# Three narrow products of a decoder kernel, with the narrow operand loaded in four quarters of TensorE's columns

## The chip, the cores and the metric

The kernel runs on one core of a Trainium2 chip, in one launch, in float32 almost throughout. The metric is the device time of an execution in microseconds (us). Three executions of the kernel before took 2194.0, 2196.74 and 2199.11 us; the median is 2196.74 us.

TensorE (PE in the profile) holds one operand of a matmul as weights and streams the other past it. VectorE is DVE, ScalarE is ACT, GpSimd is POOL, and SP is the engine whose queue issues most DMAs. A float32 matmul of this kernel leaves two records of PE in the trace, each with its own load of weights (PEld); a transpose through PE leaves one.

## The reference, cut to what matters

The decoder has two layers of three blocks, each followed by a residual sum and a layer norm. x is 8 x 256 x 512, that is 2048 tokens of 512 features. The change touches three products with a very narrow operand:

```python
# L0_attn: differential attention; one mean square per token and head, 16 heads of 32 features
attn = attn1 - lambda_full * attn2
attn = attn * jax.lax.rsqrt(jnp.mean(attn * attn, axis=-1, keepdims=True) + EPS) * ln_w
attn = attn * (1.0 - LAMBDA_INIT)
return attn @ Wo.T

# L0_ffn: mixture of experts, 8 experts, the best two of each token
logits = h @ router_w.T                      # 512 -> 8
vals, idx = lax.top_k(softmax(logits), 2)

# L1_ffn: attention with one key and value head chosen for each token, 16 heads
gating = jax.nn.softmax(x @ W_gate.T, axis=-1)   # 512 -> 16
idx = jnp.argmax(gating, axis=-1)
k_shared = jnp.einsum('bth,bthd->btd', indicator, k)
```

Between them stand a long convolution (L0_xattn), a causal attention in chunks (L1_attn) and a cross attention (L1_xattn), which the change leaves alone.

## The kernel before, in words

Tokens lie in 16 tiles of 128 (`x[t]`), features in four blocks of 128 (KB = 4). A product with 512 features is four matmuls that add up in PSUM, one for each block of features. Where tokens are to be the output's partitions, the transposed tokens are the weights and the other operand is streamed; this is how the three narrow products are done before: 128 tokens are loaded as weights, and 4, 8 or 16 columns are streamed.

The stages follow each other: differential attention (to about 486 us), long convolution (to 786), experts (to 1132), the self attention (to 1504), cross attention (to 1847), routed attention (to the end).

**The order in the two attention stages.** `causal_attention` (L1102 on) writes the order of PE, DVE, ACT and POOL out by hand. Its unit of work is one batch of 256 tokens and four heads. For each unit, PE makes scores (`ps_q`, L1158), ACT copies them (L1167), POOL masks them (L1169), DVE takes the row maxima (L1178); nine or five units later PE makes the scores again, transposed (`ps_k`, L1221 and L1230), ACT takes the exponential (`pT`, L1238), POOL masks (L1239) and adds (L1249), and PE multiplies by the values and by ones (`ps_pv`, L1264 and L1274); DVE takes the reciprocal of the sums (`rsum`, L1282) and multiplies (L380, L383 or L1288). The two kinds of scores share one PSUM tile (tag sc), so PE may start the next `ps_q` only when ACT has taken the exponential of the last `ps_k`. Between these, `fill` puts in pieces of other work up to a budget, at costs written into the code (0.86 for a 128x512 product's matmul, 0.45 for four transposes, 0.4 for a set of norm sums): projections, and what `finish` hands in after each batch. A slot's places are "start", then `ps_q`, a first fill, `ps_pv`, "mid", `ps_k`, two more fills, the row maxima on DVE, and "end".

**The head norms** are in `finish` of the differential attention (L435). For the first seven of the eight batches, ACT squares the gathered output (L480), and `norms(i)`, one for each of the two token tiles, makes four matmuls of 128 tokens by the 4 columns of `quad` (L449; `quad` has a one for each of the four groups of 32 features). DVE scales and adds epsilon into `rr` (L453), POOL takes the power -1/2 (L461), ACT widens (L457), PE transposes it (`pt_rr`, L471), DVE multiplies (L477). The last batch goes another way (L392), which is not changed.

**The routing logits** are in `token_tile` (L727) of `route`. Tokens are routed in two halves of eight tiles. For a tile, four transposes (`pt_c`, L731), an ACT copy (L737), the moments on DVE and POOL, the norm of the tile before, and four matmuls of 128 tokens by 8 router columns into `ps_r` (`project`, L172), with an ACT copy into `raw` (L744). `choose`, `send` and `table` then pick the experts, scatter the tokens and make the table of blocks. The first half runs in the middle of the long convolution, where the tile framework's scheduler sets the order; the second runs among the first three blocks of the experts (L1019 on), in an order written by hand. `ps_r`, `pt_c` and the blocks' own transposes (L195) share the two buffers of the pool `ps_t`.

**The gates** of the routed attention are in `gates` (L1698): for each group of four token tiles, 16 matmuls of 128 tokens by 16 columns of W_gate into `ps_g`, then a DVE copy (L1706), the softmax and the choice of the head (L583 to L605, L1710). Ahead of them `turned_group` transposes the group's tokens into `xT`, tile by tile (`pt`, L195; copies by ACT, L196). The `key` of each token block needs the choice.

## Time and profile before

| | |
|---|---|
| median of the runs, us | 2196.74 (2194.0 to 2199.11) |
| the profiled execution, us | 2205.52 |
| its span, first to last instruction, us | 2203.7 |
| mean granted TensorE clock | 0.971 |
| PE busy, us (share of the span) | 2054.0 (93%) |
| DVE, POOL, ACT busy, us | 1275.9, 826.9, 605.1 |
| PE's records of `ps_ss` (L449), `ps_r`, `ps_g` | 112, 128, 128 |

The profile is of one execution. A line of its lists has the source line, engine, operation, output and inputs by their names in the program, and shapes; times in the lists by time are start and duration in us, and what stands in brackets is idle time of that engine before the instruction and what ended it. A matmul's duration is longer than its distance from the next, since matmuls are pipelined; costs of PE are therefore read as distances between starts. In lists by stage, "PEclk" is the granted share of TensorE's clock.

### The profile page before, as it was taken

The page shows a single profiled execution, that of the slowest core. Times are in us where ns is not written, and L with a number is a line of the kernel's source. Part 1 is how long each engine was busy: PE and PEld are TensorE (multiplying, and loading weights), DVE is VectorE, ACT ScalarE, POOL GpSimd, SP SyncE. Part 2 cuts the span into 40 slices and gives each one's busy share as a digit, 9 for nine tenths or more (in the row PEclk, how much of TensorE's full clock was granted, in tenths as well). Part 3 has the DMA queues.
Part 4 walks back from the last instruction along what each step waited for, and adds up shares of the span by engine and source line. Part 5 has one row for each costly group of instructions (what it writes and reads, how often), then busy time and mean ns, then how long its engine had stood idle before and what let it go on. Part 6 is the DMA issues. An engine that isn't in the chain of part 4 may idle for free. (4 is left out here: it accounts for less than half of the span.)

```text
span 2203.7 us, 36445 instructions
## 1 busy us (share of the span) xinstructions
PE 2054.0 (93%) x15296; PEld 1264.8 (57%) x15296; DVE 1275.9 (58%) x1923; ACT 605.1 (27%) x773; POOL 826.9 (38%) x918
## 2 busy tenths in 40 slices
PE   8989999889999998999968999999999999999995
PEld 6646655544453464555545665656877875545543
DVE  4677777658888962222235756556344343576777
ACT  4545555410010021111113333330110110333342
POOL 2667777646557622000034544333000000142343
PEclk9989999989999999999979999999999999999998
DMA  6899802235133153131141201002100100000000
GB/s 220 331 384 381 311 1 69 78 93 186 34 115 120 29 172 121 60 144 63 43 144 30 77 20 58 2 1 96 36 22 20 39 0 1 1 11 11 11 18 32
DMA packets 110035, 197.61 MB, mean 90 GB/s; under 512 B 7088, under 2 KB 30768, under 8 KB 109872
## 3 DMA queue, kind: packets, MB, share of 16 engines
q1 hardware_dynamic: 104752, 178.49, 23.3%
q0 software_dynamic: 5120, 16.78, 2.2%
q8 instruction: 123, 2.02, 0.4%
q14 instruction: 40, 0.33, 0.0%
HBM read 93.54 MB, written 112.20 MB: 93 GB/s over the span
## 5 line engine op out<-in xcount | busy, mean ns | idle before, releaser
L1282 DVE RECIPROCAL rsum<-ps_pv 128x256 f32<-128x256 f32 x128 | 224.5, 1754 | 243.7 <-PE ps_pv L1274 243.4
L172 PE MATMUL ps_y<-kv,wt 128*128 128x512 f32 x640 | 281.1, 597 | 4.5 <-POOL kv L526 3.8
L1238 ACT ACTIVATE pT<-ps_k 128x1536 f32<-128x1536 f32 x128 | 185.8, 1451 | 286.0 <-PE ps_k L1230 282.1
L1178 DVE TENSOR_REDUCE neg<-rows 128x12 f32<-128x1536 f32 x128 | 223.0, 1742 | 54.1 <-POOL rows L1169 54.0
L1169 POOL TENSOR_SCALAR_AFFINE_SELECT rows<-rows 128x1024 f32<-128x1024 f32 x128 | 141.5, 1105 | 246.8 <-ACT rows L1167 246.5
L1167 ACT COPY rows<-ps_q 128x1536 f32<-128x1536 f32 x128 | 184.3, 1440 | 179.4 <-PE ps_q L1158 130.2
L1239 POOL TENSOR_SCALAR_AFFINE_SELECT pT<-pT 128x1024 f32<-128x1024 f32 x128 | 141.1, 1103 | 242.6 <-ACT pT L1238 242.4
L172 PEld LDWEIGHTS ps_y<-kv,wt 128*128 128x128 f32 x640 | 120.3, 191 | 153.6 <-issue 135.2
L1249 POOL TENSOR_TENSOR pT<-pT 128x512 f32<-128x512 f32 x112 | 145.7, 1301 | 9.3
L183 PE MATMUL ps_f<-xT,w_l1a 128*128 128x256 f32 x512 | 129.2, 400 | 12.2 <-ACT xT L196 12.2
L1084 POOL DMA_INDIRECT w_l1x<-ys,slots x32 | 32.7, 1023 | 279.8 <-DMA ys<-y_m 272.1
L183 PE MATMUL ps_t<-w_l1f,xT 128*128 128x512 f32 x256 | 121.9, 611 | 0.0
L183 PEld LDWEIGHTS ps_f<-xT,w_l1a 128*128 128x128 f32 x512 | 96.9, 197 | 33.8 <-ACT xT L196 14.3
L999 PE MATMUL po_m<-dn,hT 128*128 (+1 forms) x216 | 104.4, 621 | 12.0 <-ACT hT L992 10.5
L140 POOL TENSOR_SCALAR rstd<-bn_mv 128x1 f32<-128x1 f32 x80 | 16.6, 207 | 216.2 <-DVE bn_mv L146 208.1
L1274 PE MATMUL ps_pv<-pT,ones_v 128*32 128x256 f32 (+1 forms) x1152 | 84.7, 376 | 7.2 <-POOL pT L1249 7.0
L564 DVE TENSOR_REDUCE yc<-z 128x64 f32<-128x512 f32 x128 | 86.1, 674 | 6.2 <-POOL w_l1a L565 5.7
L981 DVE TENSOR_TENSOR h_b<-h_b,pg 128x352 f32<-128x352 f32 x36 | 18.8, 521 | 101.3 <-ACT h_b L980 101.3
L1158 PE MATMUL ps_q<-kz,qT 32*128 32x128 f32 x1536 | 62.2, 292 | 15.2 <-ACT pT L1238 13.3
L1158 PEld LDWEIGHTS ps_q<-kT,qT 32*128 32x128 f32 x1536 | 49.2, 188 | 44.4 <-issue 21.2
L1158 PEld LDWEIGHTS ps_q<-kz,qT 32*128 32x128 f32 x1536 | 49.8, 190 | 41.0 <-ACT pT L1238 26.2
L183 PE MATMUL ps_f<-xT,w_l 128*128 128x256 f32 x256 | 71.2, 406 | 0.9 <-POOL w_l L273 0.7
(326 smaller groups left out, 3768.7 us busy)
## 6 DMA issues: line engine op xcount, KB each, us to landing
xs<-zero SPq DMA_DIRECT2D x8, 4352.0 KB
ys<-zero SPq DMA_DIRECT2D x8, 4352.0 KB
filters<-in_L_xattn_k SPq DMA_DIRECT2D x4, 2560.0 KB
first_h<-xs SPq DMA_DIRECT2D x36, 256.0 KB
ys<-y_m SPq DMA_DIRECT2D x36, 256.0 KB
gu<-in_L_ffn_gate_up_proj SPq DMA_DIRECT2D x3, 2816.0 KB
wt<-filters SPq DMA_DIRECT2D x32, 256.0 KB
x<-in_x SPq DMA_DIRECT2D x16, 256.0 KB
```

The costliest lines, as they stand in the source:

```text
L172: nc.tensor.matmul(ps, lhsT=lhsT(k), rhs=rhs(k), start=(k == 0), stop=(k == n - 1))
L183: nc.tensor.matmul(ps[0], lhsT=lhsT(k), rhs=rhs(k), start=(k == 0), stop=(k == KB - 1))
L564: nc.vector.tensor_reduce(yc[:, lb], z, AX.X, ALU.add)
L999: nc.tensor.matmul(po, lhsT=hT[:m, i, :], rhs=dn[i][:m, bass.ds(e, 1), :], start=(i == 0), stop=(i == len(FCH) - 1),)
L1158: nc.tensor.matmul(block[:, s, j, :], lhsT=q(rows, c, b * S + i * P, P), rhs=k(rows, c, b * S + keys * P, P), start=True, stop=True,)
L1167: nc.scalar.copy(d.rearrange("p j s k -> p s j k"), block)
L1169: nc.gpsimd.affine_select(out=rows, in_=rows, compare_op=ALU.is_ge, fill=-FAR, base=0, pattern=[[0, 8], [-1, P]], channel_multiplier=1,)
L1178: return lambda: nc.vector.tensor_reduce(neg[u // upb % 2][:, :, :, c], d, AX.X, ALU.max, negate=True)
L1238: nc.scalar.activation(p[:, 0:3].rearrange("p j s q -> p s j q"), block, AF.Exp)
L1239: nc.gpsimd.affine_select(out=p[:, 0:2].rearrange("p j s q -> p (j s) q"), in_=p[:, 0:2].rearrange("p j s q -> p (j s) q"), compare_op=ALU ...
L1249: nc.gpsimd.tensor_tensor(p[:, 3], p[:, 1], p[:, 2], ALU.add)
L1282: nc.vector.reciprocal(r, ps[:, 1, :])
```

## The change

Each of the three products swaps its operands. The narrow operand becomes the weights, 32 columns wide, and the tokens are streamed. The four blocks of features go to four quarters of TensorE's columns and so to four quarters of the PSUM partitions (`ps[32 * k : 32 * k + 32]`), each matmul by itself instead of adding up. The sums over the blocks are made later: ACT or DVE copies the 128 rows out of PSUM, PE transposes them back to tokens, and DVE adds the four blocks (gates, logits) or picks them apart (norm sums, where the four blocks are different heads).

- Gates: one set of four 512-token matmuls for each group of four tiles, an ACT copy (`gpart`), four transposes placed after the first of the query products, and a DVE reduction. The second query product moves ahead of the key products. The budget cost is 0.86 and 0.45 in place of 0.8.
- Logits: one set for four tiles, after the fourth and the eighth tile of each half; the transposes and the reduction (`logits`) come at the start of the fifth tile and of `choose`. The 16 small copies of ACT become four of 128x512.
- Norm sums: one set of four 256-token matmuls for a batch (cost 0.7 in place of twice 0.4), DVE makes `means` in their place, and `norms` makes two transposes and a DVE copy at the "end" of the same slot. A 32-column version of `quad` (`quads`) is made by DVE for every batch.
- Where 32 columns reach past the end of a narrow operand, zeros stand behind it: a POOL memset behind the router weights, a DVE memset behind W_gate, whose load now goes ahead of the load of W_qkv on SP.

```diff
+    def columns_by_block(ps, dst, w, n, rhs):
+        for k in range(KB):
+            nc.tensor.matmul(
+                ps[32 * k : 32 * k + 32, :],
+                lhsT=w[:, n * k : n * k + 32],
+                rhs=rhs(k),
+                start=True,
+                stop=True,
+            )
+        nc.scalar.copy(dst, ps)
+
+    def sum_of_blocks(dst, pt, parts):
+        for i in range(pt.shape[1]):
+            nc.tensor.transpose(pt[:, i, :], parts[:, i * P : (i + 1) * P], ident)
+        n = dst.shape[2]
+        nc.vector.tensor_reduce(
+            dst, pt.rearrange("p t (k r n) -> p t r n k", k=KB, n=n)[:, :, 0], AX.X, ALU.add
+        )
...
-            def norms(i):
-                ps = pools.tile([P, H0], F32, tag="mm", name="ps_ss")
+            quads = work.tile([P, 32], F32, tag="quads", name="quads", bufs=1)
+            nc.vector.tensor_copy(
+                quads.rearrange("p (r t) -> p r t", r=8), quad.unsqueeze(1).broadcast_to([P, 8, 4])
+            )
+            means = work.tile([P, S], F32, tag="means", name="means", bufs=1)
+            def sums():
+                ps = pools.tile([P, S], F32, tag="mm", name="ps_ss")
                 for k in range(KB):
                     nc.tensor.matmul(
-                        ps[:, 4 * k : 4 * k + 4], lhsT=sq[:, k, i * P : (i + 1) * P], rhs=quad, start=True, stop=True
-                    )
-                rr = small.tile([P, H0], F32, tag="rr", name="rr")
-                nc.vector.tensor_scalar(rr, ps, 1.0 / 32, EPS, ALU.mult, ALU.add)
+                        ps[32 * k : 32 * k + 32, :],
+                        lhsT=quads,
+                        rhs=sq[:, k, :],
+                        start=True,
+                        stop=True,
+                    )
+                nc.vector.tensor_scalar(means, ps, 1.0 / 32, EPS, ALU.mult, ALU.add)
+                at(0, "end", norms)
+            def norms():
+                pt = pools.tile([P, 2, P], F32, tag="mm", name="pt_ss")
+                for i in range(2):
+                    nc.tensor.transpose(pt[:, i, :], means[:, i * P : (i + 1) * P], ident)
+                rr = work.tile([P, 2, H0], F32, tag="rrs", name="rr")
+                nc.vector.tensor_copy(
+                    rr.rearrange("p i (k t) -> p i k t", k=KB),
+                    pt.rearrange("p i (k r t) -> p i k r t", k=KB, t=4)[:, :, :, 0],
+                )
+                roots(0, rr[:, 0, :])
+                at(apart, "end", lambda: roots(1, rr[:, 1, :]))
...
-            for i in range(2):
-                at(1 + apart * i, "fill", [(0.4, lambda i=i: norms(i))])
+            at(1, "fill", [(0.7, sums)])
...
+                def logits():
+                    pt = ps_t.tile([P, PH // 2, P], F32, tag="tr", name="pt_r")
+                    i, rows = part.pop()
+                    sum_of_blocks(raw[:, i : i + PH // 2, :], pt, rows)
-                def token_tile(i):
+                def token_tile(i, pool):
                     b = tiles[i] // 2
+                    if i == PH // 2:
+                        logits()
...
-                    pr = ps_t.tile([P, E], F32, tag="tr", name="ps_r")
-                    project(pr, lambda k: xv[:, k, b, :], lambda k: rw[:, k, :])
-                    nc.scalar.copy(raw[:, i, :], pr)
+                    if (i + 1) % (PH // 2) == 0:
+                        j = i + 1 - PH // 2
+                        rows = pool.tile([P, D], F32, tag="rpart", name="rpart", bufs=1)
+                        columns_by_block(
+                            ps_t.tile([P, D], F32, tag="tr", name="ps_r"),
+                            rows,
+                            rows_w,
+                            E,
+                            lambda k: xv[:, k, j : i + 1, :],
+                        )
+                        part.append((j, rows))
                 def choose():
+                    logits()
...
+            def gate_parts():
+                columns_by_block(
+                    pools.tile([P, GT], F32, tag="mm", name="ps_g"), part, wg, H1, lambda k: xT[0][:, k, :]
+                )
             def gates():
-                ps = pools.tile([P, TPG, H1], F32, tag="mm", name="ps_g")
-                for ti in range(TPG):
-                    project(
-                        ps[:, ti, :],
-                        lambda k: xT[0][:, k, ti * P : (ti + 1) * P],
-                        lambda k: wg[:, k, :],
-                    )
+                pt = pools.tile([P, TPG, P], F32, tag="mm", name="pt_g")
                 gate = work.tile([P, TPG, H1], F32, tag="gate", name="gate")
-                nc.vector.tensor_copy(gate, ps)
+                sum_of_blocks(gate, pt, part)
...
-            need.append((0, [(0.8, gates)]))
+            need.append((0, [(MM, gate_parts)]))
             need.append((0, feature_block(pools, qT, xT, wqkv, 0, 0, HD1**-0.5)))
+            need.append((0, [(TR, gates)]))
+            need.append((0, feature_block(pools, qT, xT, wqkv, 0, 1, HD1**-0.5)))
```

Not shown: `roots`, which holds what was `root` and `widen` inside `norms`; the tiles with the zeros behind them and their two memsets; the order of the two loads in `routed_weights`; the pool that is passed to `token_tile`.

## Prediction

> **What bounds the kernel now.** I read the page's shares first, then busy time by stage, then the lists by time around the three products. Columns of the stage table: stage, length, busy us of PE, PEld, DVE, ACT, POOL, granted clock, DMA share, GB/s.
>
> ```profile
> PE 2054.0 (93%) x15296; PEld 1264.8 (57%) x15296; DVE 1275.9 (58%) x1923; ACT 605.1 (27%) x773; POOL 826.9 (38%) x918
> ...
> 300.00:432.00 132.00, 119.81 (x1686) 74.64 (x1689) 100.02 (x114) 72.16 (x73) 94.55 (x91) 0.99 0.19 58
> 630.00:650.00 20.00, 19.43 (x118) 13.95 (x117) 15.19 (x34) 6.02 (x16) 9.06 (x19) 1.00 0.37 125
> 650.00:700.00 50.00, 45.28 (x104) 18.67 (x103) 43.88 (x124) 0.26 (x1) 31.56 (x37) 0.97 0.47 164
> 786.00:860.00 74.00, 61.49 (x277) 41.48 (x275) 33.34 (x109) 20.85 (x45) 23.99 (x33) 0.93 0.60 199
> 1910.00:2130.00 220.00, 213.16 (x1989) 112.95 (x1989) 151.05 (x212) 75.48 (x76) 78.57 (x79) 0.98 0.03 11
> ```
>
> PE is busy 91 to 97% in these stages, so it sets the end and time off it counts, with two reserves. In 650 to 700 DVE is at 88% and PE idles nearly 5 us: just behind the first half's logits DVE sets the pace. And PE takes its work in order: a new instruction that waits holds all behind it.
>
> **What comes off PE.** A narrow product costs its weight loads:
>
> ```profile
> 792.01 0.60 PE L731 MATMUL pt_c<-ident,w_l1a 128*128 128x128 f32 x4
> 792.45 0.96 PE L172 MATMUL ps_r<-rw,w_l1a 128*128 128x8 f32 x8
> 793.33 0.66 PE L731 MATMUL pt_c<-ident,w_l1a 128*128 128x128 f32 x4
> ```
>
> Four matmuls (eight records) hold PE from 792.45 to 793.33: 0.88 us, or 0.81 where the list shows a product next. Norm sums: 14 sets of about 0.91, 12.8 us. Logits: 8 x 0.81 = 6.5 us in the first half, 8 x 0.86 = 6.9 in the second. Gates: 3.59 us for each group, but 6.56 for the first (1847.14 to 1853.70), which ran at half rate.
>
> **What goes on.** The kernel already has matmuls in column quarters, at L1264 and L1274:
>
> ```profile
> 265.18 0.63 PE L195 MATMUL pt<-ident,x 128*128 128x128 f32 x4
> 265.74 0.86 PE L1264 MATMUL ps_pv<-pT,v 128*32 128x256 f32 x16
> 266.42 0.61 PE L1274 MATMUL ps_pv<-pT,ones_v 128*32 128x256 f32 x8
> 266.96 0.71 PE L1221 MATMUL ps_k<-qT,kz 32*128 32x256 f32 x8
> ```
>
> Eight records of 256 columns take 0.54 us from L1274's start to the next line's, where full-array records of 512 columns stand 0.43 apart (256: 0.215): the four quarters run together, 2 x 0.215 = 0.43, and 0.11 goes to leaving the mode. Entering costs as much: the transposes end at 265.18 + 4 x 0.11 = 265.62, L1264 starts 0.12 later. So a set costs 0.66 us at 256 tokens and 0.12 + 2 x 0.43 + 0.11 = 1.09 at 512; a transpose 0.11.
>
> [...]
>
> **Gates.** The old product could start on the first tile of `xT`; the new one streams all four and waits for the last copy:
>
> ```profile
> 1909.68 2.05 ACT L196 COPY xT<-pt 128x512 f32<-128x512 f32 x4
> 1910.32 0.66 PE L195 MATMUL pt<-ident,x 128*128 128x128 f32 x4 [0.57 <-ACT xT L196]
> 1910.81 3.74 PE L172 MATMUL ps_g<-w_l1f,xT 128*128 128x16 f32 x32
> 1914.40 3.68 PE L183 MATMUL ps_f<-xT,w_l1f 128*128 128x512 f32 x8
> ```
>
> ACT ends at 1911.73; with 0.1 to hand over PE starts about 1.05 us later than now. New: 1.05 + 1.09 + 4 x 0.11 = 2.58 for 3.59, a gain of 1.0 in three groups. The first saves about 2.5 us at half rate, but what follows then sits in the same slow stretch: 1.3. Sum 4.3. The ACT copy (0.59, as L737's) is covered: between the product and the transposes PE has a query product of 3.5 us. The reduction reads 256 elements (0.41 for 0.22, by L869's 128x240), two products ahead of its first user. Without these covers a group would cost about 1.1 more.
>
> **Logits, second half** (PE's order is by hand). The first three tiles and block 1's transposes lose three sets, but then four ACT copies of 0.59 follow each other through two PSUM buffers: PE gets through in about 2.55 where it took 4.90 (792.01 to 796.91): 2.35. In the next stretch the transposes of the four-tile set stand right behind it. [...] The row agrees: the copy of 166 ns becomes one of 590, and PE waits 0.2 + 0.59 + 0.1 = 0.9. With it the stretch takes 4.75 of 4.90. The last has block 3's transposes for cover: 3.75 of 3.99. Sum 2.7; by PE's time alone it would be 6.9 - 2 x 1.09 - 8 x 0.11 = 3.8.
>
> **Logits, first half.** 6.5 - 3.1 = 3.4 us of PE. But DVE, full from 650 to 690, still has its work: it can be early only by its own idle time before, 5 us in 628 to 651, most of it waiting for copies of the tiles. Bounds 0 and 3.4; I take half, 1.7. The scatter on POOL that follows `choose`, and the 3.75 us for which PE waits on POOL at 697 (its `kv`, L526), move with it.
>
> **Norm sums.** New on PE: 0.66 + 2 x 0.11 = 0.88 for each of seven batches, 6.1 for 12.8. But between the set and its transposes lies `means` on DVE (128x256 out of PSUM; nearest row L380, 0.42). In the changed program's order PE has a whole unit in between in batches 0 and 1, one quarter of a product (0.43) in 2 and 3, and nothing in 4, 5 and 6. DVE stands in its long reciprocal:
>
> ```profile
> 318.34 0.71 PE L1221 MATMUL ps_k<-qT,kz 32*128 32x256 f32 x8
> 318.47 1.76 DVE L1282 RECIPROCAL rsum<-ps_pv 128x256 f32<-128x256 f32 x1 [2.60 <-PE ps_pv L1274]
> 319.54 1.45 ACT L1238 ACTIVATE pT<-ps_k 128x1536 f32<-128x1536 f32 x1 [1.91 <-PE ps_k L1230]
> 320.33 0.95 PE L449 MATMUL ps_ss<-quad,w_l 128*128 128x4 f32 x8
> 320.53 0.42 DVE L380 TENSOR_TENSOR yT_b<-ps_pv,rsum 128x256 f32<-128x256 f32 x1 [0.30 <-PE ps_o L183]
> 321.21 0.95 PE L1158 MATMUL ps_q<-kz,qT 32*128 32x128 f32 x24
> ```
>
> A set from 320.3 ends near 321.0; DVE is free at 320.95; `means` is there at 321.6, the transposes run from 321.8. PE waits 0.8 to 0.9, and behind it stand the next unit's scores, then ACT's copy, POOL's mask and DVE's maxima. Batches 3, 4, 5: 0.9 each; 2: 0.55; 6, which also has a norm of 0.54 ahead on DVE: 1.5. Sum 4.75. So 12.8 - 6.1 - 4.75 = 1.95, less 1.0 in batches 0 and 1, where PE waits for ACT's exponentials anyway: 1.0. DVE's own extra (`quads`, `means`, copy: about 0.5 a batch) lies in its idle quarter.
>
> **The rest.** The DVE memset behind W_gate stands in the last norm of self attention, for which PE's transposes wait: -0.2 (0.15 to 0.2, as L879's). POOL's memset (about 0.2) is hundreds of us early; the two weight loads change places at 1504 and are used at 1847.
>
> **Sum.** 4.3 + 2.7 + 1.7 + 1.0 - 0.2 = 9.5 us. The profiled execution took 2205.5 us (span 2203.7 and 1.8 around it), so about 2196. The runs' median is 2196.7, 8.8 below it; less 9.5 that is **2187 us**.
>
> **Rivals.** What a measurement can tell from no change is 0.2%, 4.4 us.
> - A, the waits vanish: PE's waits at the norms lie under ACT's exponential (it ends at 320.99 above, and the next scores can't start sooner), and DVE follows in the convolution. Norms 6.5, first half 3.4: 4.3 + 2.7 + 3.4 + 6.5 - 0.2, 17 us, 2180. Against it: DVE's 100% after 660.
> - B, no change: DVE takes all of the first half's gain, the norms gain nothing, the gates' wait is 1.5 and the second half gains 1: about 3.5, 2193. For it: four of the five places already end on another engine.
> - C, slower: at the seven `means`, DVE has the maxima (1.75, waiting on POOL's mask) ahead too. Each wait becomes 3 us, 21 in place of 4.75, 6.8 above before: 2203.5. It turns the sign from a mean wait of 2.0 us: (4.75 + 9.5)/7. Against it: in the order, the reduction stands behind `means` in six of seven batches.
> - D, the change doesn't do what it says: quarters run one after the other with 512 columns. A set costs 3.7 (2.0 at 256): gates +7, logits +4, norms +7, 2214. Against it: L1274, at 256.
>
> **Chances.** Likeliest 0.50, A 0.20, B 0.17, C 0.11, D 0.02. The likeliest alone: 2182 to 2194, as the first half goes from 0 to 3.4, the norms from -1 to 4, and the scheduler's new order around POOL's wait by 2 either way. From A's middle to short of C's: 2178 to 2202. Faster by more than 4.4: 0.42 + 0.20 + 0.02 = 0.64; within: 0.08 + 0.13 = 0.21; slower: 0.02 + 0.11 + 0.02 = 0.15.
>
> **What would show it.** `ps_g` starts some 1 us after the last transpose, waiting for ACT's `xT`, and takes 1.1 to the next product. `pt_r` in the fifth tile of the second half has 0.9 of idle before it, from ACT. `pt_ss` has five waits for DVE of about 0.9. DVE has less idle time in 628 to 651, and PE more after. I am wrong if sets of 512 do not overlap, if the `pt_ss` waits differ much from 5 us, or if a stall that is not of these places (10.5 us at 849, 17.2 at 1132) moves.

## The result, and the profile after

The changed kernel took 2173.04 us (median of 4 runs, 2169.99 to 2175.78) beside 2195.37 us for the kernel before (4 runs, 2191.62 to 2199.11): ratio 0.9905, 95% interval 0.9881 to 0.9930, 22 us faster. The forecast was 2187, with a range from 2178 to 2202. The direction was right; the size was more than double the 9.5 us of the sum, and the time lies 5 us below the range.

The profiled execution took 2173.6 us (span 2171.9). Its share of PE, and the stages that were shown of before (columns: stage, length, busy us of PE, PEld, DVE, ACT, POOL, granted clock, DMA share, GB/s); the stages are the same work, earlier by what was gained ahead of them:

```profile
PE 2019.9 (93%) x15094; PEld 1221.9 (56%) x15094; DVE 1275.8 (59%) x1935; ACT 606.5 (28%) x765; POOL 826.5 (38%) x919
```
```profile
300.00:425.00 125.00, 110.42 (x1574) 67.30 (x1573) 90.71 (x103) 68.10 (x70) 87.62 (x83) 0.97 0.21 61
...
624.00:644.00 20.00, 18.93 (x84) 9.08 (x82) 17.66 (x39) 5.57 (x10) 9.45 (x21) 1.00 0.61 205
644.00:780.00 136.00, 128.76 (x303) 56.24 (x304) 119.82 (x241) 1.71 (x3) 85.48 (x97) 1.00 0.21 70
780.00:835.00 55.00, 53.22 (x223) 32.71 (x222) 31.73 (x108) 18.65 (x36) 22.95 (x33) 1.00 0.73 244
...
1883.00:2098.00 215.00, 206.00 (x1950) 104.24 (x1954) 149.97 (x214) 77.78 (x78) 78.13 (x79) 0.99 0.03 11
```

PE is still what bounds the kernel: 93% busy, 34 us less of it. One number tells that the instructions' prices are not all: the mean granted clock is 0.980 for 0.971; in the last row it rose from 0.98 to 0.99, in the one with the second half of the logits from 0.93 to 1.00 (there with a stall that this profile doesn't have; more below).

The second group's gates by time (start, duration in us; in brackets idle time of the engine and what ended it):

```profile
1881.72 2.04 ACT L218 COPY xT<-pt 128x512 f32<-128x512 f32 x4
1882.34 0.66 PE L217 MATMUL pt<-ident,x 128*128 128x128 f32 x4 [0.56 <-ACT xT L218]
1883.81 1.06 PE L178 MATMUL ps_g<-xT,w_l1f 128*32 128x512 f32 x8 [0.81 <-ACT xT L218]
1884.81 3.70 PE L205 MATMUL ps_f<-xT,w_l1f 128*128 128x512 f32 x8
```

From `ps_g` to `ps_f` 1.00 us (0.996 from the starts of the records), with 0.81 of waiting for the last copy of `xT` ahead: both as forecast (1.09 and 1.05), a little smaller. Four quarters of 512 columns do run together.

The logits of the second half:

```profile
792.02 1.06 PE L178 MATMUL ps_r<-w_l1a,rw 128*32 128x512 f32 x8
793.79 0.66 PE L190 MATMUL pt_r<-ident,rpart 128*128 128x128 f32 x4 [0.71 <-ACT rpart L185]
794.28 0.60 PE L789 MATMUL pt_c<-ident,w_l1a 128*128 128x128 f32 x4
```

The wait for ACT's copy is 0.71 us (forecast 0.9). And the norms' sums of the seventh batch, where DVE's queue is the longest:

```profile
413.40 1.76 DVE L1349 RECIPROCAL rsum<-ps_pv 128x256 f32<-128x256 f32 x1 [0.92 <-PE ps_pv L1341]
413.85 0.64 PE L478 MATMUL ps_ss<-w_l,quads 128*32 128x256 f32 x8
...
415.19 0.42 DVE L402 TENSOR_TENSOR yT_b<-ps_pv,rsum 128x256 f32<-128x256 f32 x1
415.54 0.54 DVE L155 TENSOR_SCALAR x<-res,bn_mv,rstd 128x512 f32<-128x512 f32 x1
415.99 0.42 DVE L485 TENSOR_SCALAR means<-ps_ss 128x256 f32<-128x256 f32 x1
416.46 0.69 PE L491 MATMUL pt_ss<-ident,means 128*128 128x128 f32 x2 [1.97 <-DVE means L485]
```

`means` stands behind the reciprocal, the product and a norm, and PE waits 1.97 us for it. The seven waits are 0, 0, 0.01, 0.10, 0.55, 0.64 and 1.97: 3.3 us in all, where the forecast had 4.75.

So the steps are there as written, most within some tenths (the last norm wait, forecast at 1.5, is the largest miss). Their sum is not the result. Between the two first profiles lie 31.8 us, and at the places of the change only part of them. The experiments ask where the rest is from.

### The profile page after: what moved, and what is told of

Same layout as the page of the kernel before. It is cut to its first block, busy times and chain, and to the rows that moved or that the text cites. A ratio compares the mean times of both kernels' runs of the same rounds, so it can differ in the third digit from the quotient of the medians.

```text
span 2171.9 us, 36045 instructions
## 1 busy us (share of the span) xinstructions
PE 2019.9 (93%) x15094; PEld 1221.9 (56%) x15094; DVE 1275.8 (59%) x1935; ACT 606.5 (28%) x765; POOL 826.5 (38%) x919
## 5 line engine op out<-in xcount | busy, mean ns | idle before, releaser
L1234 ACT COPY rows<-ps_q 128x1536 f32<-128x1536 f32 x128 | 184.1, 1438 | 173.5 <-PE ps_q L1225 122.7
L1288 PE MATMUL ps_k<-qT,kT 32*128 32x256 f32 (+1 forms) x1024 | 68.4, 354 | 3.4 <-ACT rows L1234 2.2
## 6 DMA issues: line engine op xcount, KB each, us to landing
xs<-zero SPq DMA_DIRECT2D x8, 4352.0 KB, 31.8
```

The costliest lines, as they stand in the source:

```text
L1234: nc.scalar.copy(d.rearrange("p j s k -> p s j k"), block)
L1288: nc.tensor.matmul(block[:, s, at, :], lhsT=k(rows, c, b * S + j * P, P), rhs=q(rows, c, b * S + j * P, P * (2 - j)), start=True, stop=False,)
```

## The experiments

**How stages are compared.** PE's order outside the change is the same in most of the program, so the start of one and the same PE instruction can be looked up in every profile, and a stage is the distance between two of them. A stage is named by the times of its two instructions in the second profile of the kernel before ("1508 to the end", for instance, starts at 1508 there and near 1526 in the first). Stages that no change touches agree between profiles to some hundredths (150.95 to 150.97 us from 854 to 1005 in all eighteen), so a tenth of a microsecond can be read where the total varies by 5 or more. All tables below are worked out so.

**The kernel before again, and one part at a time.** First the kernel before, unchanged:

> The kernel before once more, unchanged, for a second profile of it. In the first one some 19 us of the 32 between the two profiles lie where the change touches nothing: 2.3 in the first 15 us, 3.5 at 115 to 131 (granted clock 0.73 for the next 19 us), 11 at 838 to 849, 2.6 at 1132 to 1165. Theory 1 (those are of that one execution): this profile has less than 2 us of idle PE at 838 to 849, its span is 2192 to 2197, and the rest shows where the 22 us of the medians are. Theory 2 (they belong to the kernel before): the stall of about 10 us is here again, in the same place. The ratio is 1.000 either way.

2192.23 us, ratio 1.0012 (0.9991 to 1.0033). PE's stall at 838 to 849 is not in this profile: the stage from 815 to 849 takes 33.96 us where it took 46.87. The forecast's base, the first profile at 2205.5, held one stall of 10.5 us that this execution doesn't have. With its span of 2190.2 the difference to the changed kernel's profile is 18.3 us.

Then each of the three parts alone, the other two as before. In words: the gates' product and order (`gate_parts`, `gates`, the weights' loads); the logits (`token_tile`, `logits`, `choose`); the norms (`sums`, `norms`, `roots`). The lines that mark each:

```diff
 # gates only
-            need.append((0, [(0.8, gates)]))
+            need.append((0, [(MM, gate_parts)]))
 ...
 # logits only
-                    project(pr, lambda k: xv[:, k, b, :], lambda k: rw[:, k, :])
+                        columns_by_block(ps_t.tile([P, D], F32, tag="tr", name="ps_r"), rows, rows_w, E, ...)
 ...
 # norms only
-                at(1 + apart * i, "fill", [(0.4, lambda i=i: norms(i))])
+            at(1, "fill", [(0.7, sums)])
```

> Only the gates are changed. By the forecast's steps: 1.0 us in three groups and 1.3 in the first, 4.3 us, ratio 0.998. The trace of the changed kernel gives about 4 at these places. Theory 2 (a stall elsewhere was removed) gives nothing more here, since the gates stand after all the other places: at most 6 us. Theory 3 (any change of the program's length shifts what else stalls): another 5 to 12 us of gain or loss, in places that have no gates.

> Only the routing logits are changed. By the forecast's steps 2.7 + 1.7 = 4.4 us; the trace of the changed kernel gives about 2 for the first half and 3.2 for the second: 5 us, ratio 0.9977. Theory 2 (the stall at 838 to 849 belongs to the old order of the second half, and goes with it): 15 to 17 us, ratio 0.993. Theory 3: anything from -7 to +17, with the difference in places without logits.

> Only the head norms' sums are changed. By the forecast's steps a gain of 1.0 us; the two traces from 131 to 430 us give a loss of about 1 us: ratio 0.9995 to 1.0005. Theory 2: the same, nothing at 838. Theory 4 (PE gains its 6.5 us, and the 3.5 us at 115 to 131 are the norms' own): a gain of 4 to 7 us, ratio 0.997 to 0.998, and the stretch 115 to 131 shorter than in the kernel before.

| | median, us | ratio to the kernel before |
|---|---|---|
| gates only | 2185.98 | 0.9964 (0.9940 to 0.9988) |
| logits only | 2185.95 | 0.9993 (0.9969 to 1.0017) |
| norms only | 2189.54 | 0.9992 (0.9975 to 1.0009) |

The gates alone gain 8 us (0.0036 x 2193) by the ratio, 7 by the medians, but its interval reaches from 3 to 13 us and so holds the forecast's 4.3 too. The other two can't be told from no change by their totals, and the three ratios add up to 11 us where the whole change gains about 21; executions vary too much for such sums. By stages the logits alone take 188.5 us from 620 to 815 for 192.8 to 196.4 with the old code; the norms alone 383.3 from 100 to 486 for 385.6 to 393.2. The norms' stage is shorter where a loss of 1 had been expected of the two traces. By its size that is nearer to theory 4, but the granted clock is at half for 20.5 us of this stage and for 27 to 48 us with the old code; what is left without that is worked out below.

Why the gates gain more is in the kernel before's second profile. Columns as above; the four stretches are the four groups' gates:

```profile
1820.00:1840.00 20.00, 17.51 (x66) 11.64 (x65) 7.45 (x24) 2.31 (x5) 1.48 (x4) 0.75 0.00 0
...
1890.00:1905.00 15.00, 14.44 (x102) 10.30 (x95) 5.52 (x15) 4.67 (x8) 2.36 (x2) 0.77 0.01 2
...
1975.00:1990.00 15.00, 15.00 (x82) 10.59 (x83) 6.73 (x18) 3.60 (x6) 2.87 (x3) 0.77 0.01 2
...
2060.00:2075.00 15.00, 14.78 (x81) 10.56 (x82) 6.44 (x18) 3.93 (x7) 3.21 (x3) 0.77 0.01 1
```

The granted clock is low at every one of the four, and in the last three stretches PE is never idle for more than 0.65 us (in the first once for 1.65, among the transposes). By time, for the second:

```profile
1892.48 0.66 PE L195 MATMUL pt<-ident,x 128*128 128x128 f32 x4 [0.56 <-ACT xT L196]
1892.97 5.18 PE L172 MATMUL ps_g<-w_l1f,xT 128*128 128x16 f32 x32
1897.99 5.58 PE L183 MATMUL ps_f<-xT,w_l1f 128*128 128x512 f32 x8
```

`ps_g` takes 5.02 us in place of 3.59, and the product behind it 5.51 in place of 3.61 (the second group of the first profile, at full rate). Inside `ps_g` the distance of one record from the next is 0.112 us for the first 2.0 us and 0.213 from then on: half rate, in the middle of the product. The trace's own list of the granted clock says the same: it knows only 1.0 and 0.5, each for 3.41 us or a multiple of it, and stands at 0.5 for 6.8 us from 2.0 us after the start of this `ps_g`. In five profiles with the old gates the 128 records take 17.3, 22.0, 18.5, 18.6 and 21.3 us, where 14.4 would be full rate, and 17 of the 20 group turns have a fall of the clock in `ps_g` or in the product behind it. In four profiles with the new gates (not in halves) it is 3 of 16, each in the first group. There the clock falls between 0.6 us before and 0.1 us after the start of the product, so in the first group the fall starts with the transposes and waits ahead (1.65 and 0.81 us of idle PE in the first profile of the changed kernel). In groups two to four it is 12 of 15 with the old product and 0 of 12 with the new. The transposes and waits ahead are the same or longer with the new one, so in these groups it is the narrow product that the clock falls with. The profile that the forecast was made from showed it in the first group, and in the products behind the third and the fourth, where it had not been looked for.

**The price of a set, old and new, measured by doing it twice.**

```diff
-                for ti in range(TPG):                       # old gates
+                for ti in (*range(TPG), *range(TPG)):
...
-        for k in range(KB):                                 # new gates
+        for k in (*range(KB), *range(KB)):
```

> The kernel before with each group's 16 gate matmuls made twice over, into the same place. Theory clock (the narrow product counts as low activity, so that the clock falls to half while it runs: it did so inside ps_g in one, two or four of four groups): now all four groups fall, each pass of ps_g that runs at half rate takes 6.8 in place of 3.59, ps_g takes 40 us or more in all where it took 17 to 22, and the kernel is slower by 20 to 28 us, ratio 1.009 to 1.013. Theory fixed price (3.59 a group, and a slow first group for other reasons): 4 x 3.59 = 14.4 us slower, ratio 1.0065.

> Only the gates changed, with each set of four matmuls of 512 made twice over, into the same place. Against the run with the gates alone: both theories expect 4 x 0.86 = 3.4 us more, since the mode is entered once; in the first group, which ran at half rate, up to 0.9 more. Theory clock: ps_g of groups two to four stays at full rate, 1.86 us each. If the four quarters didn't overlap, 4 x 3.4 = 14 us. Against the kernel before: 3 to 4 us faster, ratio 0.998 to 0.9987.

Old gates twice: 2224.65 us, ratio 1.0126 (1.0104 to 1.0148), 27 us slower, where the added records at full rate are worth 14.4. All four groups fall, 0.7, 1.9, 4.8 and 4.8 us after their start, and take 13.06, 12.00, 9.33 and 9.35 us: 43.7 in all for 28.7 at full rate. The third group:

```profile
1999.85 9.49 PE L172 MATMUL ps_g<-w_l1f,xT 128*128 128x16 f32 x64
2009.18 6.51 PE L183 MATMUL ps_f<-xT,w_l1f 128*128 128x512 f32 x8
```

New gates twice: 2189.77 us, ratio 0.9967 (0.9951 to 0.9984). The third group again:

```profile
1977.36 1.92 PE L178 MATMUL ps_g<-xT,w_l1f 128*32 128x512 f32 x16 [0.81 <-ACT xT L218]
1979.21 3.27 PE L205 MATMUL ps_f<-xT,w_l1f 128*128 128x512 f32 x7
```

1.855 us for two sets where one takes 0.996: a set costs 0.86, which is 2 x 0.43, four quarters at once, and 0.14 of the 0.996 is left; that it goes into entering the mode and leaving it is the author's reading (forecast 0.23). Groups two to four stay at full rate. The expected 3.4 us against the gates alone is there in `ps_g` (8.97 us in all for 4.80, the first group at half rate in both), but not in the ratio, whose interval (plus or minus 4 us) is too wide for it; the profile with the gates alone also had a fall of the clock at 1883 that this one has not, and a longer one at 2146 (10.2 us for 6.8). Theory clock holds for `ps_g` and the time; the fixed price does not. That "low activity" is the cause was the author's guess: which trait of the old product does it (few streamed columns, or new weights for every record) no run here separates.

**The change again.**

> The changed kernel once more, beside the kernel before on the same chip. The stages of the profiles so far, beside the same stages in the profiles whose code is the old one there, give norms -3.2, logits -6.5, gates -7.4, in all -17 us: ratio 0.992. Theory 1 (the parts add up, and the first 22 us were 17 and the spread of few runs): -15 to -19 us, and in the profile the norms' stages again as in the first one, to some tenths. Theory 2 (beside the parts the change takes away a stall at 838 to 849 that the old order has): -20 us or more.

2175.41 us beside 2197.40, ratio 0.9902 (0.9886 to 0.9919): the first result stands. The stages of its profile are those of the first one: norms 386.2, logits 187.5, gates 670.6. By number this is theory 2 (20 us or more); but its reason, the stall, is not what goes: see below.

**What the waits are worth.** A version with all of the change's waits moved behind other work:

```diff
-                at(0, "end", norms)
+                at(1, "mid", norms)
...
-                    if i == PH // 2:
+                    if i == PH // 2 + 1:
                         logits()
...
+        for h in range(parts):       # gates: parts = 2, each 256 tokens
             for k in range(KB):
```

> The changed kernel with its waits moved behind other work: the norms' two transposes in the middle of the next slot (waits of 0.1, 0.55, 0.64 and 1.97 before), the logits' transposes of the second half one tile later (0.71), the gate product in two halves of 256 tokens (0.81 a group, of which the second half's copy remains, some 0.4). If the waits were on the path: norms -3, logits -0.7, gates -1.6, in all -5.3 us against the changed kernel, ratio to the kernel before 0.9895. Rival (what waited then waits for the next thing: ACT's exponential in the norms, the copy of xT in the gates): less than 1.5 us in all, ratio as the changed kernel's.

2208.54 us, ratio 1.0052 (1.0031 to 1.0072), 33 us above the changed kernel: both theories missed. The waits that it was made for are gone (0.24 is left of the gates' 0.81), and two stages pay. The norms (100 to 486 us) take 416 us for 385. By time in the second batch:

```profile
175.30 0.18 DVE L493 COPY rr<-pt_ss 128x32 f32<-128x32 f32 x1
...
175.91 0.58 ACT L339 COPY v<-ps_v 128x512 f32<-128x512 f32 x1
176.15 3.27 POOL L507 TENSOR_TENSOR rr<-rr,neg_half 128x8 f32<-128x8 f32 x2
...
179.39 1.09 POOL L1306 TENSOR_SCALAR_AFFINE_SELECT pT<-pT 128x1024 f32<-128x1024 f32 x1
180.53 0.86 PE L1331 MATMUL ps_pv<-pT,v 128*32 128x256 f32 x16 [2.21 <-POOL pT L1306]
```

With the transposes I had moved POOL's two powers too, out of the slot's end into its middle: 3.27 us that wait for DVE and stand in front of the mask for which PE waits. Not all of the 31 us need be this wait itself: the clock is at half for 65 us of this stage, where the changed kernel's first profile has 20.5. And the first half's logits, moved by the same line, kept `choose` back: PE's waits for `kv` at 690 to 735 are 4.37 and 6.31 us. The gates in halves and the second half's logits were shorter, though: from 1508 to the end 664.5 us for 671.0, from 700 to 815 111.2 for 112.4. So those two alone, and the norms once more with the powers left at the slots' ends:

```diff
-                    if i == PH // 2:
+                    if i == PH // 2 + half:
                         logits()
...
-                at(0, "end", norms)                       # the second of the two only
+                at(apart - 1, "mid" if apart > 1 else "end", norms)
...
+                    at(0, "end", lambda: roots(0, rr[:, 0, :], 1))
```

> The changed kernel with two waits moved: the gate product in two halves of 256 tokens, and the logits' transposes of the second half (only these) one tile later; the norms as in the changed kernel. The run with all waits hidden lost 33 us against the changed kernel, all of it before 486 us (norms) and at 690 to 735 (first half's logits), while its stages with these two edits were shorter: from 1508 to the end 664.5 for 670.8, from 700 to 815 111.2 for 112.4. If stages add up: 7.5 us below the changed kernel, about 2168 where that is 2175, ratio to the kernel before 0.986 to 0.988. If the clock's fall only moves to another place: 3 us or less, ratio 0.989 to 0.990.

> The same, and for the first six batches the norms' two transposes in the middle of the next slot, but POOL's powers still at the ends of slots, behind the slot's masks. Two explanations of what the run with all waits hidden lost in the norms, some 4 to 6 us a batch: (a) POOL's two powers (3.27 us) stood in front of the mask that PE waited for. Then this one loses nothing and gains the waits of batches 3 to 5, 1.3 us against the previous kernel; if the two powers at the slot's end still push the next masks, 1 to 2 us a batch are lost, 6 to 12. (b) The transposes in the middle of a slot are themselves in the way of PE's next scores: then 4 us or more a batch are lost again, 25 us or more.

Ratios 0.9892 (0.9866 to 0.9918) and 0.9894 (0.9869 to 0.9919). The second loses nothing, so (b) is out and (a) is borne out: only the powers stand elsewhere in the norms, and without them in front of the mask the 4 to 5 us a batch are gone. It gains nothing either. The first was to come to 0.987 by the stages; that needs the changed kernel on the same chip, below.

**One part left out.** The same kernel (halves and late transposes in) with one part as in the kernel before: for the old norms `sums`, `norms` and `roots`; for the old logits `token_tile` and `choose`; for the old gates `gates`, the order of `need` and the weights' loads.

> The first kernel of this call with the norms' sums as in the kernel before. It tells what the norms' edit is worth when the other two are in. Forecast: 1.0 us slower than the first kernel of this call. The stages of the profiles (100 to 486 us: mean 388.7 with the old norms, 384.7 with the new): 4.0 us slower, with up to 2 either way from where the clock falls.

> The first kernel of this call with the routing logits as in the kernel before. Forecast: 4.4 us slower than the first kernel of this call. The stages of the profiles (620 to 815 us: mean 195.4 with the old logits, 187.9 with the new, 1.2 less with the late transposes): 8.7 us slower, of which the second half 3.5 and the first half, with its wait for POOL and the clock behind it, 5.

Old norms: 2185.43 us for 2182.15, 3.3 slower (ratio 0.9916, 0.9890 to 0.9943). Old logits: 2191.66, 9.5 slower (ratio 0.9931, 0.9906 to 0.9956). Both lie nearer to the stages' numbers (4.0 and 8.7) than to the forecast's (1.0 and 4.4), but the intervals of the ratios overlap with that of the full version (0.9866 to 0.9918), so the totals alone do not decide it. The gates, and the versions side by side:

> The changed kernel on the same chip as the three that follow. Its execution should agree with the earlier ones stage by stage (norms 384 to 386 from 100 to 486 us, logits 187.5 to 189, gates 670 to 672 from 1508 to the end) and differ from them, if at all, by the stall of 10.5 us at 838 to 849, by the chip.

> The gate product in two halves and the late transposes of the second half's logits, now beside the changed kernel on the same chip. By the stages: gates 3 to 6 us shorter, logits 0.5 to 1.2: ratio to the kernel before 0.002 to 0.003 below that of the changed kernel. If chips and not stages made that difference: the same ratio.

> The same and the norms' transposes in mid slot, with POOL's powers at the slots' ends. By the stages of its first profile 2.5 us less than the previous kernel (381.6 for 384.1 from 100 to 486 us), most of it where the clock didn't fall; by the timing beside it nothing (0.6 us less). Expected: 0 to 3 us.

> The second kernel of this call with the gates as in the kernel before: what the gates' edit, with its halves, is worth when the other two are in. By the forecast's steps 4.3, and about 2 for the halves: 6 us slower than the second kernel. Theory clock: the work saved is 4 x (3.59 - 1.45 - 0.44) = 6.8 us at full rate, and the falls of the clock in and behind the old product cost 2 to 8 more, where the tail does not take them back: 9 to 14 us slower, with ps_g at half rate in one to four groups of its profile.

| | median, us (lowest, highest) | ratio to the kernel before |
|---|---|---|
| changed kernel | 2186.15 (2184.13, 2188.82) | 0.9910 (0.9890 to 0.9929) |
| halves, late transposes | 2183.18 (2181.49, 2184.55) | 0.9894 (0.9875 to 0.9912) |
| and norms in mid slot | 2183.99 (2182.49, 2186.33) | 0.9898 (0.9879 to 0.9917) |
| halves, late transposes, old gates | 2197.31 (2191.59, 2204.66) | 0.9965 (0.9947 to 0.9983) |

Old gates cost 14.1 us, at the upper end of theory clock; all four groups of its profile fall (`ps_g` 5.97, 4.92, 5.38 and 4.99 us). The stretches of the four groups in the profile of the changed kernel that ran beside it (`ps_g` at 1839.35, 1898.5, 1976.4 and 2059.3), and the one between in which the clock falls:

```profile
1820.00:1840.00 20.00, 15.96 (x56) 7.49 (x55) 9.03 (x19) 3.13 (x6) 2.97 (x8) 1.00 0.00 0
1840.00:1860.00 20.00, 20.00 (x53) 9.05 (x50) 8.52 (x20) 2.04 (x4) 0.00 (x0) 1.00 0.00 1
1880.00:1890.00 10.00, 8.07 (x67) 4.31 (x67) 6.96 (x10) 3.25 (x3) 2.60 (x3) 0.83 0.00 0
1890.00:1905.00 15.00, 13.62 (x96) 7.05 (x95) 5.45 (x6) 5.44 (x8) 2.77 (x3) 1.00 0.01 2
...
1975.00:1990.00 15.00, 14.19 (x114) 7.29 (x115) 7.76 (x20) 5.11 (x9) 2.89 (x3) 1.00 0.00 1
...
2060.00:2075.00 15.00, 15.00 (x111) 7.77 (x108) 7.82 (x20) 4.93 (x6) 2.19 (x2) 1.00 0.01 1
```

Where the kernel before showed 0.75 to 0.77 around the four groups, all is 1.00, and one stretch of 0.83 stands in another place. The version with halves is 3 us below the changed kernel, its slowest run hardly above the other's fastest; the ratios' intervals overlap, so it is the best of all that ran, by about what can be told apart. It was to be 7.5 below, and by the later expectation 0.002 to 0.003 in the ratio; it is 0.0016. The norms in mid slot are worth nothing.

**The stall at 838 to 849.** Eighteen profiles have the stage from 815 to 849: nine at 34.0 us, nine at 45.7 to 47.2. The nine long ones are the first profile of the kernel before and all eight of the last two sets of kernels that ran together, with old or new logits, gates and norms; the kernels of the two sets before have none of them, one set on the same chip as a later one. In one of the long ones:

```profile
839.79 0.37 ACT L1059 COPY hT<-pt_m 128x256 f32<-128x256 f32 x1 [10.25 <-remote]
...
840.21 2.08 PE L1066 MATMUL po_m<-dn,hT 128*128 x2 [10.46 <-ACT hT L1059]
```

PE's idle time there is 10.46 or 10.47 us in the three where it was read, while POOL issues the scatters. Theory 2 of the first experiment is out: in the four later sets the stall goes by the sitting, not by the kernel; beside those eight the kernel before took 2204.5 and 2207.8 us, beside the others 2192.8 and 2197.4. The first profile of the kernel before does not fit so well: it has the stall, and the runs beside it (2191.6 to 2199.1) lie where kernels without it do. What the stall waits for, the traces do not say.

## Why the prediction was wrong

Where the gain is, by stages (means over all profiles with the old and with the new code in the stage; the versions with halves, late transposes or norms in mid slot are left out of the row that they touch), and by leaving the part out:

| part, stage | forecast | old, us | new, us | gain | left out | at half rate, old to new, us | gain at equal half rate (standard error) |
|---|---|---|---|---|---|---|---|
| norms, 100 to 486 | 1.0 | 388.7 (7 profiles, 385.6 to 393.2) | 384.8 (8, 383.3 to 387.4) | 3.9 | 3.3 | 35.6 to 22.6 | -0.3 (0.6) |
| logits, 620 to 815 | 4.4 | 195.5 (7, 192.8 to 196.4) | 187.8 (4, 187.5 to 188.5) | 7.7 | 9.5, with about 1 for the late transposes | 8.8 to 0.9 | 4.0 (0.4) |
| gates, 1508 to the end | 4.3 | 680.3 (5, 677.8 to 685.8) | 670.0 (4, 667.8 to 671.0) | 10.3 | 14.1, with about 3 for the halves | 43.0 to 30.6 | 5.6 (1.1) |
| sum | 9.5 (with -0.2) | | | 21.9 | | 87.4 to 54.1 | 9.3 |

21.9 is the measured 20 to 22 (ratios 0.9905, 0.9902 and 0.9910). The gain adds up from the three parts; nothing else is needed.

**What the forecast left out.** The last two columns split the gain. The first is the time for which the trace's clock stands at 0.5 in the stage, a mean over the same profiles. The second is what is left of the gain when a straight line (0.32, 0.47 and 0.38 us of stage for each us at half rate) is fitted through the stage lengths, with one step between old and new code. At equal half-rate time the parts gain 9.3 us, where the forecast has 9.5: the prices of instructions and waits came out nearly right in sum, in part by luck, since the norms give nothing and the gates more. The other 12 to 13 us go with 33 us less at half rate, a term that the forecast had in the first group of the gates alone, at 0.3 us (1.3 in place of 1.0). The timed runs, each with its own mean granted clock, say the same: fitted in this way the gates alone gain 4.5 us, the logits alone 4.9, the norms alone lose 0.8, and the whole change gains 9.3 and 7.2 in its two repetitions. This is a fit to executions as they came. That the change itself takes the falls away is shown by experiment for the gates (the product made twice); for the norms and the logits it rests on these counts.

**Gates: the step that failed.** "3.59 us for each group, but 6.56 for the first" took the price of one execution for the price. At full rate the old product costs 3.59 and the new one, with its wait and its transposes, 0.81 + 1.00 + 0.44 = 2.25, a gain of 5.4 us for four groups, in place of the 4.3 that the sum had. That is the small part of the error. The large part is the clock: the old product lost between 3 and 8 us by itself at half rate, and what follows it another 5 to 8 (half of the half-rate time in `ps_f`); the new one loses 0 to 3 in all. "What follows then sits in the same slow stretch" was wrong as well: the half-rate stretch of the first group lasted 10.2 us in all five profiles with the old product, and 6.8, 3.4, 3.4 us or nothing with the new one. Its length differed with the work that stood in it. Of work and clock together, some 15 us, the stage kept 10: the clock falls a few times elsewhere in the new order (at 1873 to 1886 and 2030 to 2047, 3.4 us each), and the tail gives back 1 to 3: from 2071 to the end the new order takes 120.7 to 122.7 us for 119.0 to 119.8, of which 0.5 are the gates' own transposes; where the rest goes stays open.

The row that this bears on stood in the prediction (1847.14 to 1853.70, half rate), put down as a fixed fact. What the traces show is a step (0.5, for 3.41 us or a multiple) at a varying place (0.3 to 4.7 us after the start of `ps_g`), so the question would have been how often the other three groups fall. PE had no idle gap above 1.65 us in these stretches, and in three of the groups none above 0.65; its clock fell in or right behind 32 records that stream 16 columns each.

**Logits.** Second half: 2.7 was forecast; profiles in which the clock doesn't fall take 114.5 us from 700 to 815 before and 111.8 to 112.4 after, 2.1 to 2.8. In five of seven old profiles it falls there, at 795 to 815 (116.2), in none of the new ones. The wait was 0.71 and not 0.9. First half: PE gains its 3.4 us by 650 and loses 2.8 of it by 690, as the forecast had it of DVE. What it missed comes then. The scatter on POOL starts 2.2 us earlier, counted from the instruction at 620, and PE's wait for POOL's `kv` behind it ends 1.65 us earlier; before (second profile of the kernel before) and after:

```profile
670.74 1.26 POOL L789 DMA_INDIRECT xs<-xn,slots  x1 [0.72 <-DVE slots L785]
...
691.71 0.74 POOL L565 TENSOR_TENSOR w_l1a<-r,yc 128x256 f32<-128x256 f32 x1
```
```profile
694.10 2.08 PE L172 MATMUL ps_y<-kv,wt 128*128 128x512 f32 x2 [3.73 <-POOL kv L526]
696.39 6.93 PE L172 MATMUL ps_y<-kv,wt 128*128 128x512 f32 x11 [0.22 <-DVE kv L526]
```
```profile
666.46 1.26 POOL L856 DMA_INDIRECT xs<-xn,slots  x1 [0.19 <-DVE slots L852]
...
688.03 0.74 POOL L610 TENSOR_TENSOR w_l1a<-r,yc 128x256 f32<-128x256 f32 x1
```
```profile
690.42 7.99 PE L172 MATMUL ps_y<-kv,wt 128*128 128x512 f32 x18 [2.69 <-POOL kv L571]
```

The wait shrinks from 3.73 to 2.69, and the seven records behind it, 6.5 us with a short wait among them and about half rate (most 0.85 to 1.02 from one to the next), run at 0.43 to 0.54 each. The forecast named this wait ("move with it") and gave it no price. From 690 to 700 PE takes 10.0 to 10.2 us in six of the seven profiles with the old code (9.1 in the first) and 6.0 in the three of the changed kernel (7.7 with the logits alone). The clock has its part in it: behind a wait of 3.7 us it is at half in all seven, for 3.4 or 6.8 us, and behind one of 2.7 us in four of ten, for 3.4.

**Norms.** The waits were 3.3 for 4.75, mainly none in the third and fourth batch (0.01 and 0.10 for 0.55 and 0.9); the sets and transposes cost about 6.8 us for 6.1. That makes a gain of about 2.7 before what the first two batches were thought to lose. They lose nothing: from 100 to 200 us the eight profiles with the new code take 95.0 to 99.8 us, mean 97.6, the seven with the old 98.5 to 104.1, mean 100.3. The clock is at half there for 8.1 us in the mean with the new code and 13.2 with the old; by the fit above 1.1 us of the 2.8 remain without it (standard error 0.3), where the forecast had a loss of 1.0: "where PE waits for ACT's exponentials anyway" had the wrong sign. In the rest of the stage, from 200 to 486, the same fit leaves a loss of 1.5 (0.8), where the waits and prices say a gain; why stays open. So the 3.9 us of the norms came with the clock, and the forecast's 1.0 was not far off what the instructions themselves gave.

**The rivals.** D is out (0.86 us a set). C, waits of 2 us and more, came true in one batch of seven. B, gains taken by other engines, was right of the stretch to 690 and, at equal half-rate time, of the norms. A has the nearest number (2180), not by its mechanism: three norm waits stayed, and PE's gain in the convolution came by way of POOL. What the forecast had no case for is the clock. It treated the granted clock as a property of a stretch that the change leaves as it is, and a range made of such cases could not reach 2173.

**The base.** The first profile was 8.8 us above the median and held the stall of 10.5; the forecast took the difference of sum and median, not of profiles, so this did no harm. Its "PE is busy 91 to 97% in these stages" passes over the row from 786 to 860, where it is 61.49 of 74.00 us, 83%; that row holds the stall.

## What to carry to other kernels

Before a narrow product is costed from one execution, look up its row's clock at every place where it stands, and take a second profile: here the clock fell to 0.5 in the product of 16 streamed columns or right behind it at 17 of 20 places. Making it twice cost 27 us for 14.4 us of added records, and replacing it gained about twice what the instructions alone save. Compare stages between two starts of the same instruction, since totals vary by more than the parts, and count each stage's time at half rate before its gain is put down to instructions. And when work is moved past a wait, list every engine's share of it: here two powers on POOL that went along made the stage 31 us longer, where the waits were worth 3.

## What the runs showed of the hardware

- PE's granted clock is 1.0 or 0.5 in these traces, for 3.41 us or a multiple. It fell to half (0.112 to 0.213 us a record) 0.3 to 4.7 us after the start of a run of 128x128 weights with 16 streamed columns, during which PE was not idle: at 17 of 20 such places (13 in the product, 4 right behind it), and at 3 of 16, all in the first group, where the same product streams 512 columns past 32.
- Those records start 0.112 us apart at full rate with 16 streamed columns as with 8, and so do their loads of weights: at full rate the product's time is that of its loads (32 x 0.112 = 3.58 us, measured 3.59).
- Behind a wait of PE of 3.7 us for `kv` the clock was at half in seven of seven profiles, behind one of 2.7 us in four of ten.
- Four matmuls in column quarters of 512 float32 columns take 0.86 us as one of 512 columns does on the full array (2 x 0.43); of the 0.996 us from a single set to the next product 0.14 are left, put down to entering and leaving this mode.
- POOL's power of 128x8 elements takes 1.65 us, where its mask of 128x1024 takes 1.10.
- A stall of PE of some 10.5 us (10.47 in the first profile, where ACT idles 8.94 and DVE 5.72), while POOL issues its 16 scatters, is in that profile, in all eight of two sets of kernels that ran together and in none of two other sets. What it waits for is open.
